# Graph attention layers on one core: transfers taken off GpSimd, and the last product's rows finished at other steps

## The chip, the core and the metric

The kernel runs on one core of a Trainium2 chip. The metric is device time in microseconds (us) of one execution, from start to end; smaller is better. The engines of the core are named as the profile names them: PE (TensorE, matrix products and transposes), DVE (VectorE, elementwise work), ACT (ScalarE, activations and scaled copies), POOL (GpSimd) and SP (SyncE, which here only issues transfers). SP, ACT and POOL can each issue DMA transfers; an engine takes its instructions in order, so a transfer that has to wait holds up what stands behind it on that engine.

## The reference

Two layers over a graph of 3327 nodes with 512 features. The adjacency is used three times: added to the attention scores (twice, as spatial and as edge encoding), and as A2 = adj + I in two products.

```python
h = jnp.maximum(_layernorm(x), 0.0)                    # layer 0
q, k, v = h @ Wq.T + bq, h @ Wk.T + bk, h @ Wv.T + bv
a = q @ k.T / sqrt(512) + adj + adj
x = x + softmax(a, axis=-1) @ v
h = jnp.maximum(_layernorm(x), 0.0)                    # layer 1
A2 = adj + eye
d = diagonal(A2) ** -0.5
temp = A2 @ h @ W.T
x = x + relu((d[:, None] * A2 * d[None, :]) @ temp)
```

## The kernel before

Rows are padded to 26 tiles of 128. All matrix work is in 32-bit floats, and all large products use a scheme of seven block products in place of eight: sums and differences of the blocks are formed first (DVE), seven products are accumulated in seven PSUM banks (PE), and the results are combined afterwards (DVE). The kernel has these stages.

- **Projection** (0 to about 100 us). x is loaded tile by tile (L275), normalised, and its ReLU `ht` is stored as `rowd[0]` (L324) and transposed on PE. The query side is projected and stored as `qd` (L362).
- **Scores** (about 100 to 640 us). Four groups of 13 steps. A step loads two tiles of adjacency, `g`, for the step after the next (L418), runs seven products for its pair of tiles (L454), adds them to twice the adjacency (L458, L466), and takes the exponential on ACT (L461, L468). Beside this, DVE forms the sums of adjacency for the next step (L440), which are stored as `sumd` (L446), and block sums of the exponentials of the step before, which are stored as `pd` in four pieces (L462, L481, L485, L490). The tiles `g` are reused after four steps, so a load must wait until these stores have landed. The order on DVE, PE, POOL and SP is held to that of the program by `in_order`. At the end the row totals are stored (L514) and loaded again in another layout (L573).
- **Three products** (about 640 to 2190 us), numbered g = 0, 1, 2: exponentials times h, A2 times the second h, A2 times temp. A product consists of seven block products r in the order p5, p1, p6, p7, p2, p3, p4. Each goes over two strips s of output columns, 14 and 12 tiles wide, and each strip over seven steps t: six with a pair of row tiles (L801) and a seventh with the one left over (`t is None`, L793). That makes 294 steps, about 5.4 us each, and `number_of(g, r, s, t)` is a step's number. `Step.load` fetches left tiles three steps ahead, `Right.load` the rows of the right side five steps ahead. After the sixth step `Gather.first` copies a bank to SBUF on ACT (L829) and combines four banks on DVE (L830 to L833); after the seventh `Gather.rest` adds the others (L846 to L849, or L843 for the very last strip), and `Gather.settle` folds the strip into the output `cts` (L857 to L862).

The work beside the products hangs on step numbers: `at(k, what)` puts a task into `between`, and `within` holds tasks that run inside a step after its fourth matmul. Tasks whose name contains "load" run at the beginning of the step. These tasks matter here:

- `Job` (L872 on) forms more sums of adjacency and stores them (L887); `Right.make` stores a part of the right side for later use (L766).
- `attend` and `attended` finish the rows of layer 0: they store the residual `x1d` (L907) and the second h, `rowd[1]` (L913). `Temp.product` makes temp and stores it as `rowd[2]` (L963).
- `finish` writes the result of one tile of rows: four transposes from `cts` into a bank (L987), a ReLU with scale on ACT (L989), the residual added on DVE (L990), and the store (L92). `finish_load` fetches the residual from `x1d` (L970), and `last_load` does it for the last rows (L977). All of these transposes but the last go to one bank, the role "p8", so a transpose must wait until ACT has emptied it. Rows 0 to 19 are finished whole during the block products p3 and p4 of the last product. Rows 20 to 25 are finished in halves: the second half of their columns early in block product p2 (step (4, 0, t)), the first half after everything else.

In the kernel before, POOL issues all stores but four of the last. The residual buffers come from a ring of four (`xr_ring`), the output buffers from one of four (`out_ring`).

Of the kernel before, what the change touches and what calls it, by code (L numbers as in the profile page):

```python
# [47 lines left out]
def graph_layers_kernel(  # L48
# [41 lines left out]
    def store(dst, src, n, queue=nc.gpsimd):  # L90
        for a, z in pieces(n):
            queue.dma_start(dst[a:z], src[a:z])  # L92
# [223 lines left out]
    def h_transposed(k):  # L316

        a, n = PACKS[k]
        for _, i in (o for o in order if o[0] == k):
# [4 lines left out]
            nc.gpsimd.dma_start(rowd[0][ROW[i]], ht)  # L324
# [13 lines left out]
    def project_q(k):  # L338
# [5 lines left out]
        def chain(o):  # L344
# [12 lines left out]
            def last():  # L357
                if o == 1:
                    for j in range(4):
                        y, z = divmod(j, 2)  # L360
                        i = ROW[y * HALF + a] * P
                        nc.gpsimd.dma_start(qd[:, 2 * z : 2 * z + 2, i : i + w], qs[j][:, :, :w])  # L362
# [58 lines left out]
    class Pair:  # L421
# [11 lines left out]
        def sum_of_adjacency(self, m):  # L433
# [11 lines left out]
            if m == 1:  # L445
                nc.gpsimd.dma_start(self.to(sumd)[:, 0:2], self.o)  # L446

        def multiply(self, qt):
# [8 lines left out]
            def first(n, ps, sign):  # L457
                nc.vector.scalar_tensor_tensor(a[n], a[n], 2.0, ps[:, :wd], op0=ALU.mult,  # L458
                                               op1=ALU.add if sign > 0 else ALU.subtract)
                if n == 2:  # L460
                    nc.scalar.activation(g[1], g[1], AF.Exp, **({"bias": pad} if self.t == HALF - 1 else {}))  # L461
                    nc.gpsimd.dma_start(self.to(pd)[:, 0:2], g[1])  # L462
# [15 lines left out]
        def s1(self):  # L478
            s1 = self.g[0][:, 1]
            nc.vector.tensor_add(s1, s1, self.g[1][:, 1])  # L480
            nc.gpsimd.dma_start(self.to(pd)[:, 2:4], self.g[0])  # L481

        def s2(self):
            nc.vector.tensor_add(self.e[:, 1], self.g[0][:, 0], self.g[0][:, 1])
            nc.gpsimd.dma_start(self.to(pd)[:, 4:6], self.e)  # L485

        def s4(self):
            self.last = fours[:, self.t % 2, : self.wd]
            nc.vector.tensor_add(self.last, self.e[:, 1], self.g[1][:, 0])
            nc.gpsimd.dma_start(self.to(pd)[:, 6], self.last)  # L490
# [11 lines left out]
        def total(self, m, own=None):  # L502
# [11 lines left out]
            nc.gpsimd.dma_start(totd[:, c0 : c0 + self.wd], row)  # L514
# [55 lines left out]
    def totals():  # L570
        for m in range(2):
            pairs[len(steps_of_scores) - 1].total(m, bank(ROLE["p8"], "tot"))
        nc.sync.dma_start(tot, totd[0].rearrange("(i p) -> p i", p=P))  # L573
# [110 lines left out]
    cts = {}  # L684

# [15 lines left out]
    xr_ring = ring(*spare[:3], (half, 14))  # L701
    out_ring = ring((half, 12), (half, 13), *spare[3:])
# [24 lines left out]
    class Right:  # L727
# [31 lines left out]
        def make(self):  # L759
# [3 lines left out]
            if r == "p6":  # L763
                yield nc.vector.tensor_add(own, own, self.two[:, :, 0:E])
                yield nc.vector.tensor_sub(own, own, self.two[:, :, E:D])
                nc.gpsimd.dma_start(self.t2[:, 0 : 2 * self.n], self.b[:, 0 : 2 * self.n])  # L766
# [39 lines left out]
    class Gather:  # L806
# [31 lines left out]
        def rest(self, ps):  # L838
            p = {k: ps[k][:, : self.width] for k in ("p2", "p3", "p4", "p8")}
            if self.last:  # L840
                flags.append(nc.values_load(bad, min_val=0, max_val=1))  # L841
                for o, k in zip(self.parts(self.regions[2]), p):
                    nc.vector.tensor_add(o, o, p[k])  # L843
# [25 lines left out]
    class Job:  # L869
# [13 lines left out]
        def make(self):  # L883
# [3 lines left out]
            nc.gpsimd.dma_start(sumd[self.s][self.j][:, 2 + self.k], self.a)  # L887
# [14 lines left out]
    def attend(i):  # L902
# [4 lines left out]
        nc.gpsimd.dma_start(x1d[i], xt)  # L907
        normed[i] = norm(xt)

    def attended(i):  # L910
        h1 = h_ring([P, D], "h1")
        nc.scalar.activation(h1, xts[i], AF.Relu, bias=normed[i][1](), scale=normed[i][0])
        nc.gpsimd.dma_start(rowd[1][i], h1)  # L913
# [13 lines left out]
    class Temp:  # L927
# [18 lines left out]
        def product(self, j):  # L946
# [14 lines left out]
            if j == len(PARTS) - 1:  # L961
                for i, ts in zip(self.its, self.to):
                    nc.gpsimd.dma_start(rowd[2][i], ts)  # L963
# [3 lines left out]
    def finish_load(i, z=(0, 1)):  # L967
        c0, c1 = z[0] * E, (z[-1] + 1) * E
        xrs[i] = xr_ring([P, D], "xr")
# [9 lines left out]
    def finish(i, z=(0, 1), spot=None, queue=nc.gpsimd):  # L979

        s, y, k = where(i)
# [3 lines left out]
        pt = bank(ROLE["p8"] if spot is None else spot, "pt")  # L985
        for d in range(c0 // P, c1 // P):
            nc.tensor.transpose(pt[:, d * P : (d + 1) * P], cts[s][y][d][:, k * P : (k + 1) * P], ident)  # L987
# [3 lines left out]
        store(out[i * P : i * P + n, c0:c1], o[:n, c0:c1], n, queue)  # L991
# [32 lines left out]
    def rows(g, k, i, *z):  # L1024
# [5 lines left out]
        else:  # L1030
            at(k - 1, finish_load, i, *z)
# [21 lines left out]
    for (n, s, t), its in {  # L1053
        (5, 1, 2): (0,), (5, 1, 3): (1,), (5, 1, 4): (2,), (5, 1, 5): (3,),
        (6, 0, 0): (4,), (6, 0, 1): (5,), (6, 0, 2): (6, 17), (6, 0, 3): (14, 18), (6, 0, 4): (15, 19), (6, 0, 5): (16,),
        (6, 1, 2): (7, 8), (6, 1, 3): (9, 10), (6, 1, 4): (11, 12), (6, 1, 5): (None, 13),
    }.items():
        for i, when in zip(its, (between, within)):
            if i is not None:
                k = number_of(2, n, s, t)  # L1060
                at(k - 1, finish_load, i)
                when.setdefault(k, []).append((finish, (i,)))
    for t, i in enumerate(range(20, NT)):
        rows(2, number_of(2, 4, 0, t), i, (1,))
    for n, i in enumerate(range(20, NT, 2)):
        at(number_of(2, 6, 1, 2) + n, last_load, i)
    for k, what in ((1, totals), (2, prepare), (6, prepared), (8, judge), (9, judged)):
# [32 lines left out]
    def run(k):  # L1100
        step = steps[k]
# [18 lines left out]
        for j, _ in enumerate(itertools.chain((None,), step.multiply(banks_of))):  # L1120
# [11 lines left out]
            elif weighs and j > 0:  # L1132
                do(first_of(waiting), 2)
        if t is None:
            do(first_of(waiting))
            gatherer.rest(banks_of)
# [13 lines left out]
    with in_order(*(e.engine for e in (nc.vector, nc.tensor, nc.gpsimd, nc.scalar, nc.sync))):  # L1150
        for k in range(len(steps)):
            run(k)
        for n, i in enumerate(range(20, NT)):
            finish(i, (0,), (0, 2, 4, 6, 7, 1)[n], (nc.gpsimd, nc.sync)[n % 2])
# [376 lines left out]
```

## Time and profile before

| What | us |
|---|---|
| median of 3 runs | 2209.17 |
| lowest and highest | 2204.41, 2212.06 |
| the profiled execution, its own time | 2208.99 |
| its span, from the first to the last instruction | 2207.1 |
| TensorE busy in the span | 2172.1 (98%) |
| VectorE busy | 1664.2 (75%) |
| ScalarE busy | 238.4 (11%) |
| GpSimd busy | 357.2 (16%) |
| mean granted TensorE clock | 0.993 of full speed |
| DMA: 583.71 MB moved, mean | 264 GB/s |

A line of instructions gives the source line, the engine, the operation, the tile written and the tiles read, and how long it took; idle time before it stands in brackets, with what ended it. A "q" behind an engine's name means its sequencer, which issues transfers and waits, and isn't counted as busy. For PE, weight loads are listed apart as PEld. An FP32 matmul of the program shows as two records. The granted clock is the share of full speed that the chip's throttle let PE have in a stretch.

### The profile page before, as it was taken

The numbers are of one execution on the slowest core, as the hardware profiler recorded it, in microseconds if no ns is written. First come the engines' busy times: TensorE is split into PE (matmuls) and PEld (weight loads), VectorE is DVE, ScalarE is ACT, GpSimd is POOL, SyncE is SP. The second block draws the span as 40 slices with busy tenths as digits, with TensorE's granted clock in tenths as the row PEclk, the third lists the DMA queues.
The fourth block names the chain that finished last, engine by engine and source line by source line (L and its number), as shares of the span: only waits on it lengthen the run. The fifth ranks groups of instructions, "written<-read, shape, count | busy, mean of one in ns | idle before, by whom it ended". The sixth has DMA issues, their size and how long they took to land. (4 is left out here: it accounts for less than half of the span.)

```text
span 2207.1 us, 21499 instructions
## 1 busy us (share of the span) xinstructions
PE 2172.1 (98%) x6424; PEld 1198.7 (54%) x6424; DVE 1664.2 (75%) x3250; ACT 238.4 (11%) x363; POOL 357.2 (16%) x551
## 2 busy tenths in 40 slices
PE   9999999999999999999999999999999999999997
PEld 6555555455545555555454555555666655555554
DVE  6369888888877788777777778886667577876775
ACT  5311121112110000000001000000111100000011
POOL 5233333333321000001222100000000000000011
PEclk9999999999999999999999999999999999999999
DMA  8568888888969898889787889886645458766684
GB/s 288 186 221 296 293 296 287 302 283 311 359 214 326 308 373 293 274 291 318 254 307 266 302 325 347 290 291 202 217 149 187 142 193 304 235 210 186 208 294 151
DMA packets 247196, 583.71 MB, mean 264 GB/s; under 512 B 34768, under 2 KB 107294, under 8 KB 247070
## 3 DMA queue, kind: packets, MB, share of 16 engines
q1 hardware_dynamic: 192782, 399.28, 53.9%
q0 software_dynamic: 44928, 167.49, 20.1%
q10 hardware_dynamic: 9360, 15.47, 2.2%
q8 instruction: 53, 0.87, 0.2%
q14 instruction: 73, 0.60, 0.1%
HBM read 414.28 MB, written 167.85 MB: 264 GB/s over the span
## 5 line engine op out<-in xcount | busy, mean ns | idle before, releaser
L801 PE MATMUL p<-part,b 128*128 128x448 f32 (+1 forms) x3528 | 1268.6, 515 | 5.0 <-DVE part L174 4.9
L801 PEld LDWEIGHTS p<-part,b 128*128 128x128 f32 x3528 | 670.4, 191 | 544.3 <-issue 287.6
L454 PE MATMUL Y<-qt,hp 128*128 128x448 f32 (+1 forms) x832 | 308.8, 513 | 2.4 <-DVE g L458 1.5
L173 DVE TENSOR_TENSOR part<-part 128x896 f32<-128x896 f32 (+1 forms) x252 | 256.8, 1019 | 61.0 <-DMA part<-p 26.4
L454 PEld LDWEIGHTS Y<-qt,hp 128*128 128x128 f32 x832 | 157.3, 190 | 137.7 <-issue 72.3
L454 PE MATMUL Z<-qt,hp 128*128 128x384 f32 (+1 forms) x416 | 162.5, 513 | 0.0
L175 DVE TENSOR_TENSOR part<-part,part 128x448 f32<-128x448 f32 (+1 forms) x219 | 129.4, 591 | 14.9
L174 DVE TENSOR_TENSOR part<-part,part 128x448 f32<-128x448 f32 (+1 forms) x219 | 129.4, 591 | 7.2
L793 PE MATMUL p<-part,b 128*128 128x448 f32 (+1 forms) x336 | 124.2, 513 | 0.0
L454 PEld LDWEIGHTS Z<-qt,hp 128*128 128x128 f32 x416 | 78.8, 190 | 67.4 <-issue 37.4
L458 DVE SCALAR_TENSOR_TENSOR g<-g,Y 128x384 f32<-128x384 f32 (+1 forms) x156 | 91.3, 585 | 29.2 <-PE Y L454 28.1
L887 POOL DMA_DIRECT2D sum<-job x52 | 28.4, 547 | 503.9 <-DVE job L884 285.9
L793 PEld LDWEIGHTS p<-part,b 128*128 128x128 f32 x336 | 63.6, 190 | 53.1 <-issue 31.3
L829 ACT COPY part<-p 128x384 f32<-128x384 f32 (+1 forms) x33 | 16.6, 503 | 669.4 <-PE p L801 669.4
L454 PE MATMUL X<-qt,hp 128*128 128x384 f32 (+1 forms) x208 | 81.1, 512 | 0.0
L461 ACT ACTIVATE g<-g 128x768 f32<-128x768 f32 (+1 forms) x48 | 43.0, 896 | 351.4 <-DVE g L458 299.3
L446 POOL DMA_DIRECT2D sum<-o x52 | 36.8, 709 | 218.8 <-DVE o L440 150.3
L92 POOL DMA_DIRECT2D out_dram<-r x30 | 16.2, 542 | 309.3 <-DVE r L990 269.0
L830 DVE TENSOR_TENSOR part<-p,part 128x384 f32<-128x384 f32 (+1 forms) x33 | 19.3, 585 | 59.5 <-PE p L801 58.8
L893 PE MATMUL p<-w,ct 128*128 128x512 f32 x136 | 61.8, 594 | 0.4 <-DVE part L905 0.4
L454 PEld LDWEIGHTS X<-qt,hp 128*128 128x128 f32 x208 | 39.5, 190 | 33.1 <-issue 19.3
L954 PE MATMUL pw<-w,rows 128*128 128x256 f32 x208 | 53.6, 380 | 0.8 <-DVE rows L944 0.8
(191 smaller groups left out, 2048.6 us busy)
## 6 DMA issues: line engine op xcount, KB each, us to landing
part<-sum SPq DMA_DIRECT2D x104, 448.0 KB, 5.2
part<-p SPq DMA_DIRECT2D x91, 448.0 KB, 6.1
part<-sum SPq DMA_DIRECT2D x104, 384.0 KB, 3.5
part<-p SPq DMA_DIRECT2D x91, 384.0 KB, 4.2
part<-in_adjT_dram SPq DMA_DIRECT2D x78, 448.0 KB, 4.7
b<-row SPq DMA_DIRECT2D x234, 128.0 KB, 4.9
part<-in_adjT_dram SPq DMA_DIRECT2D x78, 384.0 KB, 3.6
g<-in_adjT_dram SPq DMA_DIRECT2D x52, 448.0 KB, 4.4
```

What stands on the lines that cost most here:

```text
L173: yield nc.vector.tensor_add(o[:, 0:2], g[:, 0:4:3], g[:, 1:2].to_broadcast([P, 2, g.shape[-1]]))
L174: yield nc.vector.tensor_add(o[:, 2], o[:, 1], g[:, 0])
L175: yield nc.vector.tensor_add(o[:, 3], o[:, 2], g[:, 2])
L446: nc.gpsimd.dma_start(self.to(sumd)[:, 0:2], self.o)
L454: nc.tensor.matmul(ps[:, :wd], h_of(self.t, name, k), qt[B[name]][:, k], start=start and k == 0, stop=k == 1, skip_group_check=True)
L458: nc.vector.scalar_tensor_tensor(a[n], a[n], 2.0, ps[:, :wd], op0=ALU.mult, op1=ALU.add if sign > 0 else ALU.subtract)
L461: nc.scalar.activation(g[1], g[1], AF.Exp, **({"bias": pad} if self.t == HALF - 1 else {}))
L793: yield nc.tensor.matmul(ps[("p2", "p3", "p4", "p8")[k]][:, :w], b[:, z], a[:, 0, y], start=k == 3, stop=True)
L801: yield nc.tensor.matmul(ps[r][:, :w], b[:, i], m, start=self.t == 0, stop=self.t == PAIRS - 1 and r in ("p1", "p5", "p6", "p7"))
L887: nc.gpsimd.dma_start(sumd[self.s][self.j][:, 2 + self.k], self.a)
L893: nc.tensor.matmul(ps, cts[s][y][d][:, k * P : (k + 1) * P], w[d], start=d == 0, stop=d == DC - 1)
L954: nc.tensor.matmul(ps, a, W[B[name]][:, c], start=new and c == 0, stop=c == 1, skip_group_check=True)
```

## The change

- No transfer is issued by POOL any more. Stores of the projection and of the scores go to SP; stores of the products go to ACT.
- Stores of the products are not issued where they are recorded. `post` (and `finish` by itself) puts them on a list, and `deliver(k)`, called in step k after its matmuls, issues those that were recorded in steps before k. Only `attended` issues its store at once. At the end SP issues the last rows' stores, but for two that ACT issues.
- The load of the row totals is a task of its own, `load_totals`, at step 3; it stood at the end of `totals` at step 1.
- Residual buffers come from a ring of seven, output buffers from one of five, and `finish_load` runs two steps ahead of `finish` instead of one.
- The rows 0 to 19 are finished at other steps of p3 and p4 (the table of `within`), and the second half of the columns of rows 20 to 25 two steps later.
- For the last six rows, `rest` is split: the adds of p2 and p3, then the transposes of rows 20 to 22 (`turn_last`), then the adds of p4 and p8 and the transposes of rows 23 to 25. Before, all four adds came first, and each row's transposes were followed by its evictions.

The diff, cut to its core (the one-word changes of a queue's name are shown once for each target):

```diff
-    def store(dst, src, n, queue=nc.gpsimd):
+    def store(dst, src, n, queue=nc.scalar):
...
-            nc.gpsimd.dma_start(rowd[0][ROW[i]], ht)
+            nc.sync.dma_start(rowd[0][ROW[i]], ht)
...
             pairs[len(steps_of_scores) - 1].total(m, bank(ROLE["p8"], "tot"))
+
+    def load_totals():
         nc.sync.dma_start(tot, totd[0].rearrange("(i p) -> p i", p=P))
...
+    now = [0]
+    posted = []
+
+    def post(dst, src):
+        posted.append((now[0], lambda: nc.scalar.dma_start(dst, src)))
+
+    def deliver(before):
+        while posted and posted[0][0] < before:
+            posted.pop(0)[1]()
...
-    xr_ring = ring(*spare[:3], (half, 14))
-    out_ring = ring((half, 12), (half, 13), *spare[3:])
+    xr_slots = [lambda k=k: view(2, 1).rearrange("p a w -> p (a w)")[:, k * D : (k + 1) * D] for k in range(3)]
+    xr_slots = itertools.cycle([*xr_slots, *(lambda f=f, k=k: f(k, [P, D], "xr") for f, k in (*spare[:3], (half, 14)))])
+    out_ring = ring(*((half, k) for k in (11, 12, 13)), *spare[3:])
...
-            nc.gpsimd.dma_start(sumd[self.s][self.j][:, 2 + self.k], self.a)
+            post(sumd[self.s][self.j][:, 2 + self.k], self.a)
...
-        nc.gpsimd.dma_start(rowd[1][i], h1)
+        nc.scalar.dma_start(rowd[1][i], h1)
...
+    def turned(i, z, spot):
         s, y, k = where(i)
+        pt = bank(spot, "pt")
+        for d in range(z[0] * DC // 2, (z[-1] + 1) * DC // 2):
+            nc.tensor.transpose(pt[:, d * P : (d + 1) * P], cts[s][y][d][:, k * P : (k + 1) * P], ident)
+        return pt
+
+    turned_last = {}
+
+    def turn_last(i):
+        turned_last[i] = turned(i, (0,), LAST[i - 20])
+
+    LAST = tuple(ROLE[p] for p in ("p6", "p7", "p5", "p2", "p3", "p1"))
+
+    def finish(i, z=(0, 1), spot=None, queue=nc.scalar):
+
         n = min(P, N - i * P)
...
-        pt = bank(ROLE["p8"] if spot is None else spot, "pt")
-        for d in range(c0 // P, c1 // P):
-            nc.tensor.transpose(pt[:, d * P : (d + 1) * P], cts[s][y][d][:, k * P : (k + 1) * P], ident)
+        pt = turned(i, z, ROLE["p8"]) if spot is None else turned_last[i]
...
-        store(out[i * P : i * P + n, c0:c1], o[:n, c0:c1], n, queue)
+        posted.append((now[0], lambda: store(out[i * P : i * P + n, c0:c1], o[:n, c0:c1], n, queue)))
...
-            at(k - 1, finish_load, i, *z)
+            at(k - 2, finish_load, i, *z)
...
-        (5, 1, 2): (0,), (5, 1, 3): (1,), (5, 1, 4): (2,), (5, 1, 5): (3,),
-        (6, 0, 0): (4,), (6, 0, 1): (5,), (6, 0, 2): (6, 17), (6, 0, 3): (14, 18), (6, 0, 4): (15, 19), (6, 0, 5): (16,),
-        (6, 1, 2): (7, 8), (6, 1, 3): (9, 10), (6, 1, 4): (11, 12), (6, 1, 5): (None, 13),
+        (5, 1, 1): (0,), (5, 1, 2): (1,), (5, 1, 3): (2,), (5, 1, 4): (3,), (5, 1, 5): (4,),
+        (6, 0, 1): (5,), (6, 0, 2): (6, 14), (6, 0, 3): (15, 16), (6, 0, 4): (17, 18),
+        (6, 1, 1): (19, 7), (6, 1, 2): (8, 9), (6, 1, 3): (10, 11), (6, 1, 4): (12, 13),
...
-        rows(2, number_of(2, 4, 0, t), i, (1,))
+        rows(2, number_of(2, 4, 0, t + 2), i, (1,))
...
-    for k, what in ((1, totals), (2, prepare), (6, prepared), (8, judge), (9, judged)):
+    for k, what in ((1, totals), (3, load_totals), (2, prepare), (6, prepared), (8, judge), (9, judged)):
...
+        deliver(k)
         if t is None:
             do(first_of(waiting))
-            gatherer.rest(banks_of)
+            if gatherer.last:
+                flags.append(nc.values_load(bad, min_val=0, max_val=1))
+                for n, names in enumerate((("p2", "p3"), ("p4", "p8"))):
+                    gatherer.rest(banks_of, names)
+                    for i in range(20 + 3 * n, 23 + 3 * n):
+                        turn_last(i)
+            else:
+                gatherer.rest(banks_of)
...
+        deliver(len(steps))
+        now[0] = len(steps)
         for n, i in enumerate(range(20, NT)):
-            finish(i, (0,), (0, 2, 4, 6, 7, 1)[n], (nc.gpsimd, nc.sync)[n % 2])
+            finish(i, (0,), LAST[n], nc.scalar if n in (3, 4) else nc.sync)
+        deliver(len(steps) + 1)
```

## The prediction

> **What bounds the kernel now.** I read in this order: the busy shares, the stretches of the end one by one, the order of time on TensorE (PE), ScalarE (ACT) and VectorE (DVE) around each idle stretch, the waits of SyncE (SP), and the lines at which the program closes. The page first:
>
> ```profile
> span 2207.1 us, 21499 instructions
> PE 2172.1 (98%) x6424; PEld 1198.7 (54%) x6424; DVE 1664.2 (75%) x3250; ACT 238.4 (11%) x363; POOL 357.2 (16%) x551
> q0 software_dynamic: 44928, 167.49, 20.1%
> ```
>
> PE is the bound: 35 us of the span are left, 1.1 before the first matmul, 14.1 after the last transpose (2192.92), 19.7 in between. Work that PE must do isn't touched, so only these 35 us, and PE's own time at half clock, can be won; any wait that reaches PE is lost. The stretches of the end (columns: length, busy time of PE, PEld, DVE, ACT, POOL, granted clock, DMA share, GB/s):
>
> ```profile
> 1978.00:1984.30 6.30, 3.22 (x10) 1.38 (x9) 6.14 (x8) 0.00 (x0) 0.00 (x0) 1.00 0.75 259
> 1984.30:1992.00 7.70, 7.70 (x19) 3.84 (x19) 7.32 (x18) 0.78 (x2) 0.54 (x1) 0.78 0.34 105
> 2126.60:2133.50 6.90, 3.63 (x15) 2.17 (x14) 5.42 (x12) 0.69 (x1) 1.08 (x2) 0.88 0.72 216
> 2133.50:2139.50 6.00, 6.00 (x14) 2.92 (x13) 4.54 (x10) 0.69 (x1) 1.08 (x2) 0.56 0.53 166
> 2195.10:2207.10 12.00, 0.00 (x0) 0.00 (x0) 0.00 (x0) 0.00 (x0) 0.01 (x1) 0.57 0.15 44
> ```
>
> Twice PE idles and then works at a reduced clock; for the last 12 us nothing computes. The two idle stretches in order of time (in brackets: idle before, and who ended it):
>
> ```profile
> 1984.14 0.33 PE L987 MATMUL pt<-ident,part 128*128 128x128 f32 x1 [2.53 <-DVE part L859]
> ...
> 2126.43 5.36 ACTq L970 DMA_DIRECT2D xr<-x1d  x2
> 2130.75 0.68 DVE L990 TENSOR_TENSOR r<-r,xr 128x512 f32<-128x512 f32 x1
> 2131.89 0.69 ACT L989 ACTIVATE r<-pt,sd 128x512 f32<-128x512 f32 x1 [7.50 <-DVE r L990]
> 2132.63 1.12 PE L987 MATMUL pt<-ident,ct 128*128 128x128 f32 x4 [3.27 <-ACT r L989]
> ```
>
> First: a transpose of a finished row waits for the settling sums (L857-859) of that very strip. Second: ACT issues two residual loads, the second stands 5 us until DVE's add (L990) frees its buffer; the ReLU behind it on ACT is late, so the one bank for transposes stays full and PE stands. Then the waits of SP and the closing instructions:
>
> ```profile
> SPq L418 <- DMA p<-g: 441.1, 48, 48.2
> L573 SPq EVENT_SEMAPHORE  x1: 25733/25733/25733, 625.7 to 625.7; - x1
> L1523 POOLq DRAIN  x3: 40/107/5459, 2200.8 to 2206.8; - x3
> L1527 POOLq INC_SWDGE_SEM  x1: 1512/1512/1512, 2199.2 to 2199.2; - x1
> DMA to landing us min/median/max: 2.0/3.4/6.0
> ```
>
> In scores SP's loads of adjacency wait for the landing of the stores of two steps before. At the end GpSimd (POOL) alone spends 1.51 us on its counter and 5.46 us on a drain while all others stand; the last line is of the stores of the result (L92).
>
> **What the skill says.** "TensorE: Matmul & The Clock Gate", Part 1: The HAM clock gate: an idle window of about 3.4 us halves the clock, and the window runs free. The trace agrees: clock 0.56 after 3.27 us of idling, 0.78 after 0.56 and 2.53. "DMA: Bandwidth & Descriptors", SWDGE vs HWDGE vs iDMA: all issuing engines feed the same 16 DMA engines, and a separate queue saves only time at issue. The trace agrees in that a byte costs about the same from either queue: 20.1% for POOL's 167.49 MB against 53.9% for SP's 399.28 MB, so 12% more from SP. No page has a price for the drain.
>
> **The change part by part.** The order of both built programs shows 491 transfers on POOL before and none after; SP goes from 1185 to 1496, ACT from 65 to 245; the counts of arithmetic on PE, DVE, ACT and POOL are equal.
>
> 1. Rows 20-25, first columns, two steps later (t+2), loads at k-2. The settling sums ended at 1984.08; a step here is about 5.4 us, so the transposes come some 9 us after what held them. Gone: 0.56 + 2.53 = 3.09 idle, and 7.7 x (1 - 0.78) = 1.7 of clock: 4.8 us. Price if the cover fails: the same again.
>
> 2. Residual ring from 4 to 7, loads at k-2, output ring from 4 to 5, rows spread anew. A load at step k now needs the add of seven rows ago, where DVE was late by about one step; two rows a step make that over three steps. Gone: 3.27 idle, and half of the 6.1 us from 2132.63 to about 2138.7 that ran at half clock, 3.05: 6.3 us. The other waits of this kind (0.35 at 2182) add 0.3. What is late next is VectorE (9.96 of 12.9 us busy in the two stretches from 2126.6), by less than a step. If a store on ACT waits in the loads' place, one such stall returns: 6.3.
>
> 3. The last rows in halves. The last matmul ended at 2190.75 (2188.01 + 2.74), transposes began at 2191.39 after all four adds. Now the upper half's two adds are done before that matmul ends, so ACT's six evictions, 0.36 apart, start 0.64 earlier. Gain 0.6; bounds 0 and 1.0 (two adds of 0.49).
>
> 4. The close without POOL. The last store was issued at 2195.06 and landed 4.2 us later; SP's waits up to 2199.73 and its 12 waits from 2200.7 to 2201.4 would have ended it, then two barriers of together 0.8 (2206.27 to 2207.06). POOL's counter and drain stood between. After: landing, 0.5 + 0.7 + 0.1 + 0.8 = 2.1 us, against 7.8 (2199.26 to 2207.06): gain 5.7. POOL's last work is then a norm's power (L200, before 1240 us), so a drain that remains lies beside PE. If the drain must still run last, the gain is 0.3. The last landing: one such store alone took 2.08 from SP, the last of seven together 4.2; I take 3.5, gain 0.7, bounds 0 and 2.1.
>
> 5. Stores of scores on SP: five a step of 10.5 us. SP issued a load here in 0.39 us, so 2 us of issue in a queue that stood 402 of 440 us for landings. Queued behind a store that waits for DVE or ACT are the next loads (L418), and for these DVE's adjacency sums (L440), the scores' updates behind them, PE. Cover: a load issued at 303.2 landed at 307.83 and was read at 315.03: 7.2 us. The loads wait for the landing of these stores anyway, and stores stand in the program's order, before the next loads, as on POOL. DMA share: 0.83 in scores; stores are half of that, at 12% more per byte 0.88-0.89, so landings lengthen by perhaps 1 us, well inside. Cost 0; bounds -1 and +7.
>
> 6. Stores of products on ACT: 52 sums, 21 of the right side, 26 residuals, 26 + 26 rows and most of the output: some 180 x 0.33-0.45 = 70 us of issue in 1550 us in which ACT is busy for under a tenth. They're handed over a step later than computed, so their data is ready; behind them stand the copy L829, which waited 669 us for PE, and the evictions L958 and L989. Cost 0; bounds 0 and +4.
>
> 7. The totals' load two steps later: SP no longer stands 25.7 us at L573 for a landing, though it now stands for DVE's total before it can store it (649.9 against 651.4). Four idles of PE here, 0.58, 0.87, 0.96 and 0.64, are late loads and sums; I take 1.0 of the 3.05, bounds 0 and 3.
>
> 8. First stage: 26 row stores and 16 query stores on SP among the loads of x. PE idles 2.5 us in the first 100; cost 0, bounds -1 and +3.
>
> Sum: 4.8 + 6.3 + 0.3 + 0.6 + 5.7 + 0.7 + 1.0 = 19.4 us. The profiled execution took 2209.0 us, and the median of the runs is 2209.2, so no correction: 2189.6.
>
> **Rivals.**
> - The stall or the close comes back in part: one wait of point 2's kind in ACT's queue (+6.3), or the drain still last (+5.4). For it: ACT issues in order, and I can't see what the drain waits for. Against: seven slots, and no transfer of POOL is left. 2195-2196; with both 2201.
> - Lost elsewhere: points 5 to 8 at their bad bounds (7 + 4 + 1 + 3 = 15) leave 4 us: 2205, no change that can be told.
> - Slower: in scores, load, sum, store and load again now share one queue in order. It decides once a load lands over 11.8 us after its issue (315.03 - 303.2). Then each us beyond is paid in nearly every one of 52 steps: 1 us late costs some 50, less 19 won: 2240. For it: SP waits 402 us for exactly these landings, and DMA is at 0.83 already. Against: 4.6 us is what a load takes, with 7.2 to spare.
> - It isn't done: excluded by the order, no transfer is left on POOL.
>
> **How the numbers follow.** Chances: the forecast (2182-2195) 0.62, a part comes back (2195-2202) 0.20, lost elsewhere 0.07, slower 0.11. The range reaches from the sum with good bounds (landing 1.4 more, point 7 2.0, others 2-4: 2182) to the second case's end with a little of the third: 2203. About 0.3% (6.6 us) is what a measurement of this kernel can tell from no change; beyond it on the fast side lie the first two cases: faster 0.82, same 0.07, slower 0.11.
>
> **What would show it.** Right: no half clock between 1950 and 2195; under 1 us of idle of PE before any transpose of a finished row; the span ends 9 to 10 us after the last matmul (16.3 before) and POOL's long drain, if there is one, lies far earlier; scores as long as before within 3 us. Wrong: DVE's L440 waiting for g in most steps, ACT's evictions waiting behind its own stores, or POOL still closing last.

## The result and the profile after

| What | before, us | after, us |
|---|---|---|
| median of 4 runs | 2209.14 | 2187.01 |
| lowest and highest | 2204.41, 2212.06 | 2183.81, 2190.65 |
| the profiled execution, its own time | 2208.99 | 2190.65 |
| its span | 2207.1 | 2188.9 |

The ratio is 0.9902, with a 95% interval of 0.9878 to 0.9927: 22.1 us less, between 16 and 27. The prediction had 19.4 less, 2189.6. The profiled execution of the changed kernel is the slowest of its four, so a later profile of the same kernel (after_again, 2185.35) stands beside it where that matters.

The page of the changed kernel, span, busy shares and DMA queues:

```profile
span 2188.9 us, 21095 instructions
...
PE 2168.6 (99%) x6424; PEld 1198.7 (55%) x6424; DVE 1665.0 (76%) x3250; ACT 238.8 (11%) x363; POOL 48.6 (2%) x60
...
q1 hardware_dynamic: 265102, 512.76, 69.5%
q10 hardware_dynamic: 35150, 69.48, 8.7%
```

The counts on PE, DVE and ACT are what they were. POOL has lost its 491 transfers, the software queue is gone, and SP (q1) and ACT (q10) carry its bytes. The end of the last product and the close, in stretches (length, busy time of PE, PEld, DVE, ACT, POOL, granted clock, DMA share, GB/s):

```profile
1950.00:2035.00 85.00, 83.94 (x253) 46.37 (x252) 65.20 (x113) 3.86 (x8) 0.00 (x0) 1.00 0.70 218
2035.00:2120.00 85.00, 85.00 (x261) 46.89 (x260) 62.35 (x116) 5.62 (x9) 0.00 (x0) 1.00 0.78 260
2120.00:2179.12 59.12, 59.12 (x212) 34.57 (x211) 48.13 (x89) 10.60 (x16) 0.00 (x0) 1.00 0.67 230
2179.12:2188.90 9.78, 1.42 (x13) 1.06 (x10) 2.81 (x7) 2.30 (x6) 0.00 (x0) 0.82 0.28 89
```

From 2035 to the last matmul PE has no idle at all and the full clock; the only idle left there is 1.06 us at 1955, which was there before. From the last matmul to the end it takes 9.7 us (16.3 before); this stretch is called the close below. When PE reaches the same points of the program tells where the time went:

| PE reaches | before | after | after_again |
|---|---|---|---|
| the totals' matmul (L507) | 648.16 | 648.08 | 645.22 |
| the matmul of the last product's p7 that waits there | 1955.20 | 1955.68 | 1950.55 |
| the end of the last matmul | 2190.75 | 2179.12 | 2173.99 |
| the end of the program | 2207.06 | 2188.86 | 2183.57 |

In both profiles 12.1 us are won between 1955 and the last matmul, and 6.6 to 6.7 behind it. What differs between them lies before 1955: the first won nothing there, the second 4.7 us. Of these 5.1 us of difference, 2.9 lie before the totals' matmul, where the first idles 1.7 us more at 634 and has a window of 3.4 us at half clock behind that. The other 2.3 lie between 650 and 1955: another such window at 878, and 0.58 us of idle at 1339, both absent in the second.

The waits of SP that point 5 asked about, and POOL's drains at the close (x, shortest/median/longest in ns, first and last start):

```profile
SPq L418 <- DMA p<-g: 110.4, 47, 6.3
```

```profile
L1557 POOLq DRAIN  x3: 34/45/82, 1239.9 to 2188.6; - x3
```

SP stands 110 us for the landings of the stores of g instead of 441. It now issues these stores itself, and stands for their data before that instead: some 190 us at L446, L462, L481 and L485. DVE's L440 never waits for g. No drain takes longer than 82 ns.

### The profile page after: what moved, and what is told of

Same layout as the page of the kernel before. It is cut to its first block, busy times and chain, and to the rows that moved or that the text cites. A ratio compares the mean times of both kernels' runs of the same rounds, so it can differ in the third digit from the quotient of the medians.

```text
span 2188.9 us, 21095 instructions
## 1 busy us (share of the span) xinstructions
PE 2168.6 (99%) x6424; PEld 1198.7 (55%) x6424; DVE 1665.0 (76%) x3250; ACT 238.8 (11%) x363; POOL 48.6 (2%) x60
## 4 chain that ended last, share of the span: by engine, by line
PE 93%; DVE 4%; DMA 2%; issue 1%; SPq 0%; ACT 0%; POOL 0%; DVEq 0%; POOLq 0%
PE p L813 52%; PE Y L454 13%; PE Z L454 7%; PE p L805 5%; PE p L905 4%; PE pw L966 3%; PE X L454 3%; PE Y L347 2%; PE Z L347 1%; DVE part L173 1%; DMA part<-sum 1%; PE mm L306 1%; PE tp L327 1%; PE pt L995 1%; PE X L347 0%
## 5 line engine op out<-in xcount | busy, mean ns | idle before, releaser
L200 POOL TENSOR_TENSOR rstd<-ve,mhalf 128x1 f32<-128x1 f32 x52 | 42.7, 823 | 572.1 <-DVE ve L198 541.8
L896 DVE TENSOR_TENSOR job<-job 128x896 f32<-128x896 f32 (+1 forms) x52 | 53.0, 1019 | 0.0
L466 DVE TENSOR_TENSOR g<-g,Z 128x384 f32<-128x384 f32 (+1 forms) x52 | 30.5, 586 | 27.0 <-PE Z L454 26.7
```

The source lines that it names most:

```text
L896: nc.vector.tensor_add(self.a, self.a, self.b)
```

## The experiments

Twelve runs follow, eleven of other kernels and one of the changed kernel again. Times are medians of four runs (13 in one case); "chip 1", "chip 2" and "chip 3" are the three groups that shared a chip and its runs of the kernel before (medians 2207.73, 2209.68 and 2208.82).

### The two halves of the change (chip 1)

**stores_only**: the changed kernel with rings, tables, steps and the last adds as before.

```diff
-            at(k - 2, finish_load, i, *z)
+            at(k - 1, finish_load, i, *z)
...
-        rows(2, number_of(2, 4, 0, t + 2), i, (1,))
+        rows(2, number_of(2, 4, 0, t), i, (1,))
...
-                for n, names in enumerate((("p2", "p3"), ("p4", "p8"))):
-                    gatherer.rest(banks_of, names)
-                    for i in range(20 + 3 * n, 23 + 3 * n):
-                        turn_last(i)
+                gatherer.rest(banks_of)
```

> The kernel before with only its stores moved off GpSimd (SyncE in projection and scores, ScalarE in the products through the list, SyncE and ScalarE at the end); rings, tables of rows, totals' load and the adds of the last rows as before. Theory of the prediction (points 4 to 6): the close gains 6.4 us (5.7 without counter and drain, 0.7 of landing) and the queues cost nothing, so 2209.1 - 6.4 = 2202.7; both idle stretches of the last product (some 3 us each, with half clock behind) stay. Rival A, the gain of the whole change lies in the schedule and the new queues give a part back: 2205 to 2209. Rival B, the stores' queue was itself a cause of the stalls: below 2199, and the idle before the transposes at 2130 shrinks below 2 us.

**schedule_only**: the kernel before with the new steps, rings and tables, and nothing else.

```diff
-    xr_ring = ring(*spare[:3], (half, 14))
-    out_ring = ring((half, 12), (half, 13), *spare[3:])
+    xr_slots = [lambda k=k: view(2, 1).rearrange("p a w -> p (a w)")[:, k * D : (k + 1) * D] for k in range(3)]
...
+    out_ring = ring(*((half, k) for k in (11, 12, 13)), *spare[3:])
...
-        rows(2, number_of(2, 4, 0, t), i, (1,))
+        rows(2, number_of(2, 4, 0, t + 2), i, (1,))
```

> The kernel before, stores still by GpSimd, with the new steps alone: residual ring of seven and loads two steps ahead, output ring of five, the new table of rows, rows 20 to 25 two steps later, the totals' load at step 3. Theory (points 1, 2 and 7): 4.8 + 6.3 + 0.3 + 1.0 = 12.4 less, 2196.7; no idle over 1 us before a transpose of a finished row, and the close still 16 us from the last matmul to the end, with the drain of 5 us. Rival: stalls return through the output buffers, which are freed by GpSimd's slower stores: idle over 2 us before a transpose, 2202 or more.

Measured: stores_only 2196.88 (ratio 0.9943, 0.9926 to 0.9960), schedule_only 2195.87 (0.9945, 0.9929 to 0.9962). By medians 10.9 and 11.9 less: together 22.7, so within the intervals the halves add up to the whole's 22.1. The second agrees with its 12.4. From the wait at 1955 to the last matmul schedule_only takes 223.4 us, as the changed kernel does, stores_only 233.4 and the kernel before 235.5. So the 12.1 us of this stretch belong to the new steps and rings.

The first won more than the 6.4 that I had given to the stores; its interval begins at 8.8. By its time, below 2199, it went to rival B. By its trace it didn't: near 2130 it idles 4.0 us in three pieces (0.94, 2.04 and 1.03), more than the 3.27 before, though no window at half clock follows. Its trace is 10.3 us shorter than that of the kernel before: 6.5 at the close, 2.2 between 1955 and the last matmul, and 1.7 before 1955. What lies before 1955 was the next question. Its trace holds a second surprise, at the very end. Before the change (in order of time; the group of four adds brings the last four banks into the rows):

```profile
2189.37 1.97 DVE L843 TENSOR_TENSOR part<-part,p 128x384 f32<-128x384 f32 x4
...
2191.39 1.53 PE L987 MATMUL pt<-ident,part 128*128 128x128 f32 x12 [0.65 <-DVE part L843]
```

The same place in stores_only, where the four adds still stand together:

```profile
2184.79 2.10 PE L802 MATMUL p<-part,b 128*128 128x384 f32 x6
...
2185.51 1.97 DVE L852 TENSOR_TENSOR part<-part,p 128x384 f32<-128x384 f32 x4
...
2186.72 1.57 PE L992 MATMUL pt<-ident,part 128*128 128x128 f32 x12
```

The adds end at 2187.48, yet the transposes begin at 2186.72 without idle. So the 0.65 us did not hang on the order of the adds. What stores_only keeps of the change there is the list of banks: before, row 20, the first, was transposed into bank 0, where the last product's p8 lies until the fourth add has read it; `LAST` gives that bank to row 25, the last. schedule_only, which keeps the list of before, keeps the 0.65 us too. No run changed the list alone, so this cause is read from the code; that it isn't the halves is shown.

### What the drain waits for (chips 1 and 2)

**last_on_pool**, **three_last_on_pool**: one, or three, of the last stores by POOL in the changed kernel. **first_on_pool**: one early store. **scores_on_pool**: all stores of projection and scores.

```diff
-            finish(i, (0,), LAST[n], nc.scalar if n in (3, 4) else nc.sync)
+            finish(i, (0,), LAST[n], nc.gpsimd if n == 4 else nc.scalar if n == 3 else nc.sync)
```

> The changed kernel with one of the seven last stores (row tile 24) issued by GpSimd; no other transfer by GpSimd. Theory: any software transfer still open at the end brings the counter and the drain back behind the last landing: 5.4 to 7 us more than the changed kernel, 2192.5 to 2194, with a drain of about 5 us that runs last. Rival: the drain's length comes from the many transfers before (491 in the kernel before): with a single one it takes under 1 us, and the time is within 2 us of the changed kernel's 2187.

```diff
-            nc.sync.dma_start(rowd[0][ROW[i]], ht)
+            (nc.gpsimd if i == 0 else nc.sync).dma_start(rowd[0][ROW[i]], ht)
```

> The changed kernel with one early store (the first tile's h in the projection) issued by GpSimd, all else as in the changed kernel. Theory: the drain waits only for GpSimd's own work to end, so it runs near 1240 us beside TensorE: within 1.5 us of the changed kernel's 2187. Rival: counter and drain stand behind the barrier at the end whenever the program has one software transfer: 5.4 to 7 us more, 2192.5 to 2194, with the drain last.

```diff
-            finish(i, (0,), LAST[n], nc.scalar if n in (3, 4) else nc.sync)
+            finish(i, (0,), LAST[n], (nc.gpsimd, nc.sync)[n % 2])
```

> The changed kernel with the last six rows' stores given out as before the change (rows 20, 22 and 24 to GpSimd, the others to SyncE); no other transfer by GpSimd, so three in all. Theory: the long drain belongs to the many transfers that GpSimd has issued over the execution, not to late ones; with three there is no counter, the drain ends with the landing, as with one, and from the last matmul to the end it takes 8 to 10 us: time within 2 us of the changed kernel. Rival: it belongs to late software stores, and one of them was too few to show it: counter and a drain of 5 us at the end, 12.5 us or more from the last matmul to the end, 2191 or more.

```diff
-            nc.sync.dma_start(rowd[0][ROW[i]], ht)
+            nc.gpsimd.dma_start(rowd[0][ROW[i]], ht)
...
-                nc.sync.dma_start(self.to(sumd)[:, 0:2], self.o)
+                nc.gpsimd.dma_start(self.to(sumd)[:, 0:2], self.o)
...
-            nc.sync.dma_start(self.to(pd)[:, 2:4], self.g[0])
+            nc.gpsimd.dma_start(self.to(pd)[:, 2:4], self.g[0])
```

> The changed kernel with the stores of the projection and of the scores back on GpSimd, none of them later than the scores; products' and last stores as in the changed kernel. Theory: counter and long drain come back (many transfers), but right behind GpSimd's last work near 1240 us, beside TensorE, so that the close stays at 8 to 10 us and the time within 3 us of the changed kernel. Rival: they stand behind the closing wait of SyncE whenever there were many software transfers: 5 us or more after the last landing, 2192 or more.

| Kernel | transfers by POOL | longest drain behind POOL's work, us | its start | from the last matmul to the end, us | median, us |
|---|---|---|---|---|---|
| before | 491 | 5.46 (and 1.51 of counter) | 2200.8 | 16.3 | 2209.1 |
| schedule_only | 491 | 5.46 (and 1.52) | 2188.8 | 15.9 | 2195.87 |
| scores_on_pool | 310, the last at 651 | 4.89 | 1239.8 | 10.0 | 2191.94 |
| rows_of_h_on_pool (below) | 42, the last at 125 | 3.50 | 1239.7 | 10.9 | 2188.53 |
| three_last_on_pool | 3 | 2.29 | 2179.9 | 10.3 | 2185.85 |
| last_on_pool | 1 | 2.85 | 2177.1 | 10.8 | 2185.69 |
| first_on_pool | 1, the first | 0.14 | 1239.3 | 9.7 | 2187.6 |
| after | 0 | 0.08 | 2188.3 | 9.7 | 2187.01 |

The drains of scores_on_pool, and then of three_last_on_pool:

```profile
L1557 POOLq DRAIN  x3: 44/107/4892, 1239.8 to 2188.5; - x3
```

```profile
L1557 POOLq DRAIN  x3: 40/113/2286, 2179.9 to 2186.5; - x3
```

My theory for last_on_pool, that any late software transfer brings the drain back, fell. With one late store the drain ends at 2179.91, 0.1 us after that store's landing, while SP's own stores are still under way, so it isn't what ends the program. Nor is a cost shown: the closes with one or three late transfers by POOL, 10.8 and 10.3 us, lie within the 9.5 to 10.9 of the nine traces that have the changed close and no late transfer by POOL. A drain of 5 us belongs to the many transfers issued before, and stands right behind POOL's own last work: with 310 transfers it takes 4.89 us at 1240, beside PE, and costs nothing. first_on_pool went as its theory said. The kernel before had both, many transfers and a last one at the very end. Its trace shows POOL itself waiting for its landings, then the counter, and then the drain; no close of a kernel with 310 transfers or fewer has the counter.

By its time scores_on_pool went to the rival (some 6 us over three_last_on_pool and rows_slot, the kernels of chip 2 that keep all of the new schedule), by its drain to the theory: what it lost lies elsewhere, before 650 us.

### The stores of the projection (chip 3)

Without the wait for the first matmul, PE idled 5.7 us before 650 in scores_on_pool; on the same chip it was 3.2 in three_last_on_pool and 1.3 in ring_undone and rows_slot. Two of these stretches lie at 55 and 98, as in the kernel before. The kernel before in order of time:

```profile
50.76 1.24 POOL L324 DMA_DIRECT2D row<-ht  x2 [0.73 <-ACT ht L323]
...
52.02 1.08 POOL L200 TENSOR_TENSOR rstd<-ve,mhalf 128x1 f32<-128x1 f32 x2
...
52.62 0.16 DVE L204 SCALAR_TENSOR_TENSOR nb<-mv,rstd 128x1 f32<-128x1 f32 x1 [2.08 <-ACT hp L332]
...
54.50 1.06 PE L327 MATMUL tp<-ident,ht 128*128 128x128 f32 x8 [0.66 <-DVE nb L204]
```

The kernel after, at the same tiles:

```profile
51.77 0.55 POOL L200 TENSOR_TENSOR rstd<-ve,mhalf 128x1 f32<-128x1 f32 x1 [5.41 <-DVE hp L334]
...
52.35 0.16 DVE L204 SCALAR_TENSOR_TENSOR nb<-mv,rstd 128x1 f32<-128x1 f32 x1 [0.59 <-POOL rstd L200]
```

POOL computes a power for each norm (L200), and its stores stood in front of it; the norm, ht and the transposes behind it were late. (The bracket at L204 names ACT, whose copy ended at about the same time; what L204 reads is the power, which ended at 52.58.) After the change POOL is idle 5.4 us and takes the power at once. The second stretch hangs on a landing: SP's wait in scores_on_pool between 80 and 100,

```profile
SPq L399 <- DMA qd<-qs: 8.8, 1, 8.8
```

is for a store of queries that POOL issued right behind a store of sums and that landed 6.4 us after its issue. To settle the part of the projection:

```diff
-            nc.sync.dma_start(rowd[0][ROW[i]], ht)
+            nc.gpsimd.dma_start(rowd[0][ROW[i]], ht)
...
-                        nc.sync.dma_start(qd[:, 2 * z : 2 * z + 2, i : i + w], qs[j][:, :, :w])
+                        nc.gpsimd.dma_start(qd[:, 2 * z : 2 * z + 2, i : i + w], qs[j][:, :, :w])
```

> The changed kernel with the stores of the projection alone (26 of h, 16 of queries) back on GpSimd; the scores' stores stay on SyncE. Theory, new after the runs so far: GpSimd computes the power of each norm (L200) in the projection, and its own stores stood in front of it; so TensorE's busy time from 50 to 100 us falls from 49.8 back to about 48.1 with idle near 54 and 96, and the time rises by 1.5 to 2 us; the rest of scores_on_pool's loss belongs to the scores. Rival: these idles come from the DMA traffic of the scores' stores or from chance: TensorE's busy time in that stretch stays over 49.5.

| Kernel | PE busy from 50 to 100, us | idle at 54 to 56 | idle at 96 to 98 | median, us |
|---|---|---|---|---|
| before | 48.15 | 0.66 | 1.19 | 2209.1 |
| scores_on_pool | 47.98 | 0.67 | 1.34 | 2191.94 |
| schedule_only | 49.33 | 0.67 | none | 2195.87 |
| rows_of_h_on_pool | 49.33 | 0.68 | none | 2188.53 |
| after | 49.85 | none | none | 2187.01 |

Half right: the first stretch comes back with the projection's stores alone. It stands in all five traces with these stores on POOL, and in none of the nine others. The second doesn't come back: there the sums are stored by SP, the queries' store on POOL lands after 2.9 us, and nothing is late. But a store of sums by POOL in front is not enough to make it late: schedule_only has it, and the queries land after 4.1 us. A rival is that the stores wait behind SP's loads of g. In the three traces with this idle the last of these loads lands at 88.8 to 89.8, in schedule_only at 86.9, and in all four the store of sums lands 0.8 to 1.0 us behind it. No run parts the two, so the cause of the second stretch stays open.

The time rose by 3.2 us against the changed kernel on the same chip, more than these 0.7 us; the trace also shows 1.50 us of idle at 634, of which more below.

The scores' stores have a stretch of their own. In all four traces with these stores on POOL, DVE's L440 stands 3.5 to 5.6 us between 570 and 600 for transfers that haven't landed (1.80 and 1.12 for g at 575 and 577 in the kernel before), and PE idles 0.6 to 2.3 us between 575 and 610. The ten others show neither.

### Single steps of the schedule

**rows_only** (chip 3): the kernel before with one edit.

```diff
-        rows(2, number_of(2, 4, 0, t), i, (1,))
+        rows(2, number_of(2, 4, 0, t + 2), i, (1,))
```

> The kernel before with one edit: the second half of rows 20 to 25 finished two steps later. Theory (point 1): 4.8 us less than before, of which 3.1 are idle before the transposes at 1981 to 1985 and 1.7 the half clock behind it; the idle near 2130 and the close stay. Rival: VectorE is late by more than two steps there and the wait only moves: less than 2 us gained, idle over 1 us before these transposes.

Measured over 13 runs: 2203.6, ratio 0.9976 (0.9968 to 0.9985), 5.2 less. No idle over 0.25 us between 1957 and 2129; the idle of 3.28 at 2129 and the close of 16.3 stay. The wait went and nothing took its place.

**ring_undone** (chip 2): the changed kernel with both rings and the loads as before, undone together; the new table stays.

```diff
-        xrs[i] = next(xr_slots)()
+        xrs[i] = xr_ring([P, D], "xr")
...
-                at(k - 2, finish_load, i)
+                at(k - 1, finish_load, i)
```

> The changed kernel with the residual ring of four, the output ring of four and the loads of residuals one step ahead again; the new table of rows stays, and so do the stores on ScalarE. Theory (point 2): the ring and the earlier loads carry the gain, so most of 6.3 us comes back: idle of 2 us or more before a transpose of a finished row around 2130, 2191 to 2194. Rival: the new table alone spreads the rows enough, so under 1 us of idle before any transpose, and within 2 us of the changed kernel.

Measured: 2191.05, 5.2 and 5.6 over the two other kernels of chip 2 that keep the rings, three_last_on_pool and rows_slot. Its order of time:

```profile
2113.94 7.93 ACTq L981 DMA_DIRECT2D xr<-x1d  x2
...
2120.83 0.68 DVE L1012 TENSOR_TENSOR r<-r,xr 128x512 f32<-128x512 f32 x1
2121.92 0.69 ACT L1011 ACTIVATE r<-pt,sd 128x512 f32<-128x512 f32 x1 [7.30 <-DVE r L1012]
...
2122.66 1.12 PE L994 MATMUL pt<-ident,ct 128*128 128x128 f32 x4 [3.06 <-ACT r L1011]
```

It is the stall of before, link by link: the second residual load stands on ACT until DVE's add frees its buffer, the ReLU behind it is late, PE stands 3.06 us. With a second idle of 0.84 us at 2166 and half of the 3.4 us at half clock behind the stall, that makes 5.6 us. The new table alone doesn't spread the rows enough; the rival fell. What the residual ring, the output ring and the earlier loads are worth one by one was not measured.

### The idle that comes and goes, and a faster version

The profiled execution of the changed kernel idles at 634, more than before the change:

```profile
632.09 0.69 DVE L774 TENSOR_TENSOR b<-rows 128x512 f32<-128x512 f32 x1 [3.36 <-DMA rows<-row]
...
634.43 1.69 PE L454 MATMUL Y<-qt,hp 128*128 128x384 f32 x4 [2.21 <-DVE g L466]
```

DVE stands for rows of the first product's right side, with sums that PE needs behind it. The buffer of these rows is one that the last group of scores reads until about 625, so SP can load it no earlier: it issues the load between 624.1 and 625.3 in all eight traces with these buffers and SP's stores in scores. These show an idle of 2.21, 1.97, 0.50, 3.68, 1.65, 1.50 and 0.50 us, and once none. **rows_slot** (chip 2) gives the rows a buffer that is free by then:

```diff
-    b_ring = ring(*((half, k) for k in (0, 1, 2, 3, 8, 9, 10)))
-    r_ring = ring(*((half, k) for k in (4, 5, 6, 7)))
+    b_ring = ring(*((half, k) for k in (0, 1, 2, 7, 8, 9, 10)))
+    r_ring = ring(*((half, k) for k in (4, 5, 6, 3)))
```

> The changed kernel with two half-size buffers swapped: the fourth of the right side's row buffers was one that the last group of scores still reads, and is now one that is free by then (its partner goes to a buffer that no load has to wait for). Theory: the idle before a product of scores near 634 us (0.5 to 3.7 us in three looks at the same code, and half clock behind it in two of them) comes from VectorE standing for rows that SyncE could load only at 625; with the buffer free the load goes out earlier, this idle falls under 0.6, and the time falls by 2 to 4 us against the changed kernel, about 2184. Rival: the loads land late because the DMA engines are full there, whatever their issue: the idle stays 1 us or more, and the time within 1 us of 2187.

```profile
625.61 0.68 DVE L774 TENSOR_TENSOR b<-rows 128x512 f32<-128x512 f32 x1
...
630.68 1.56 PE L454 MATMUL Y<-qt,hp 128*128 128x384 f32 x4
```

DVE takes the rows at 625.6, without a wait (632.1 and 630.9 in the two profiles of the changed kernel; in the eight traces it waits 0.95 to 4.82 us), and PE has no idle over 0.25 us from 26 to 643. settle_split, which has the same buffers, shows the same. The median, 2185.48, is within what the measurement can tell from the changed kernel (2187.01, 2185.29), so the stall went and the gain of 2 to 4 us isn't shown by the times. The four runs lie within 1.8 us.

**settle_split** (chip 3) has the buffers of rows_slot and adds an edit for the idle that is left in the products: of the six settling sums after p7, three are done a step later, behind the sums of adjacency that PE needs, and a job that would fall into that step moves on by one.

```diff
-            waiting.append(gatherer.settle())
+            settle = gatherer.settle()
+            if step.r == "p7":
+                waiting.append(itertools.islice(settle, 3))
+                later.append(settle)
+            else:
+                waiting.append(settle)
```

> The changed kernel with the buffers of rows_slot, and two edits more: of the six settling sums after block product p7 three are done a step later, behind the sums of adjacency for the next product, and a job that falls into the step of these sums is moved one step on. Theory: the idle before products at 878, 1422, 1454 and 1955 (1.93, 1.06, 0.86 and 1.06 us) is VectorE's settling in front of sums that TensorE needs; all four fall under 0.3, 4.9 us less, with the rows' stall 6 to 9 less than the changed kernel on the same chip: 2178 to 2181. Rival: VectorE has no slack there and the idle only moves a step on: less than 2 us beyond rows_slot, 2183 or more.

**after_again** is the changed kernel as it is.

> The changed kernel as it is, for a comparison on one chip with the three others. Theory: 2184 to 2189, with idle near 634 us that differs from one execution to the next; from the last matmul to the end 9 to 10 us. Rival: the first measurement was of a chip that favours it, and the time is over 2191.

Measured on chip 3: after_again, as expected, 2185.29 (2183.63 to 2186.43), settle_split 2178.39 (2175.48 to 2179.47; ratio to before 0.9859, 0.9843 to 0.9875). The ranges don't overlap: 6.9 us less than the changed kernel, within what was expected, and the fastest version here. PE around the three places, first in settle_split, then in after_again:

```profile
860.00:900.00 40.00, 40.00 (x121) 22.73 (x120) 36.23 (x58) 0.48 (x1) 0.00 (x0) 1.00 0.84 287
1400.00:1460.00 60.00, 60.00 (x175) 32.76 (x174) 53.93 (x89) 0.48 (x1) 0.00 (x0) 1.00 0.87 303
1940.00:1960.00 20.00, 20.00 (x63) 11.78 (x63) 16.33 (x25) 0.48 (x1) 0.00 (x0) 1.00 0.74 230
```

```profile
860.00:900.00 40.00, 38.07 (x115) 21.45 (x114) 33.49 (x52) 0.48 (x1) 0.00 (x0) 1.00 0.83 285
1400.00:1460.00 60.00, 58.08 (x168) 31.43 (x167) 52.53 (x88) 0.48 (x1) 0.00 (x0) 1.00 0.85 295
1940.00:1960.00 20.00, 18.94 (x59) 10.91 (x58) 17.88 (x27) 0.00 (x0) 0.00 (x0) 1.00 0.63 192
```

1.93 + 1.92 + 1.06 = 4.91 us of idle are gone. Against them stand 0.63 us at 1315, which no other trace has, and 0.71 at 1332, at a matmul where seven other traces idle 0.4 to 0.8 us and after_again by chance doesn't. The two profiles are 5.9 us apart; half of 3.4 us that settle_split spends less at half clock near 25 us, which its edits don't touch, is part of that.

## Why the prediction came out

The forecast case held: 2187.0 against 2189.6. Its points, one by one:

| Point | predicted, us | what the runs show |
|---|---|---|
| 1 rows 20 to 25 later | 4.8 | 5.2 (3.3 to 7.1), rows_only |
| 2 rings, loads, table | 6.6 | 5.2 to 5.6, ring_undone (without the table) |
| 1 and 2 together | 11.4 | 12.1, from 1955 to the last matmul |
| 3 last rows in halves | 0.6 | 0.65, but not from the halves |
| 4 close and last landing | 6.4 | with point 3: 16.31 to 9.74, so 6.6 of 7.0 |
| 5 and 8 scores and first stage | 0 | 1.85 of idle gone at 54 and 96, 0.58 at 578: 2.4 |
| 6 products' stores on ACT | 0 | no loss seen |
| 7 totals' load | 1.0 | none seen |

- **Points 1 and 2** were right in mechanism and size. (Point 1 names the first columns; what moves is the second half of the columns, and its sum doesn't hang on that.) The chain of the stall was reproduced by undoing the rings and the earlier loads. Their price in half clock was an estimate on top of the idle, and that part is chance: in rows_only the same idle of 3.28 brought one window of 3.4 us at half clock, in the kernel before one of 6.8; that makes 1.7 us of difference at the same stall.
- **Point 3** was right in size and wrong in cause. It said that the upper half's adds being done early starts the transposes earlier. stores_only keeps the adds together and starts them just as early. I had read the list of banks in the diff and not asked which bank the last add still reads.
- **Point 4**: the close fell to 9.7 us, in the 9 to 10 that I gave. Of the open question, what the drain waits for, this much is answered: it is long where POOL has issued many transfers, and it follows POOL's own last work. The landing took 3.2 us (from 2183.70 to SP's wait ending at 2186.94; predicted 3.5), but the last issue was not earlier for it. SP's second store here took 1.87 us to issue, so that the last went out 4.6 us after the last matmul (4.3 before):

```profile
2178.96 1.57 PE L995 MATMUL pt<-ident,part 128*128 128x128 f32 x12
2179.38 2.30 ACT L1012 ACTIVATE r<-pt,sd 128x256 f32<-128x256 f32 x6 [6.19 <-PE pt L995]
2179.89 1.89 DVE L1013 TENSOR_TENSOR r<-r,xr 128x256 f32<-128x256 f32 x5 [0.17 <-ACT r L1012]
2180.34 2.31 SPq L92 DMA_DIRECT2D out_dram<-r  x2
```

- **Points 5 and 8** are the term that was mis-sized. I priced what SP would have to issue more, and forgot what POOL would have to issue less: its stores stood in front of the norms' powers (0.66 us), and DVE's waits for g near 575, which I had feared from SP's one queue, stood in the kernel before and went (0.58). The cause of the 1.19 us at 96 is open. With the measured sizes the sum is 5.2 + 5.4 + 6.6 + 2.4 = 19.6, and that it comes so near the forecast's 19.4 is in part luck: 2.4 that I did not foresee stand against point 7's 1.0 and 1.2 too much in points 1 to 4. With the traces' 12.1 in place of 5.2 + 5.4 it is 21.1; what is left to the medians' 22.1 lies inside the result's interval. after_again's profile, 23.5 us shorter than that of the kernel before, shows chance in the clock as well: it spends 10.2 us less at half clock, of which the 3.4 at 878 come and go.
- **Point 7** failed. The idle of 0.64 at 648 is in every trace, with the load at step 1 or 3, and schedule_only, which has the new step, keeps the idle of 0.9 to 1.0 us at 633 and 636. The idle near 632 to 636 had another cause, the buffer of the right side's rows (in the kernel before DVE waits 2.40 us for them at 630.9), which rows_slot took away.

Left open: why a store's issue on SP takes 0.35 us once and 1.87 the next time; no run was made for it. It is no accident of one execution: all eleven traces with the changed close have one issue of 1.2 to 1.9 us on SP there, the three with the old close none. In eight of them a long issue on ACT ends within 0.02 us of it, as if both queues waited for one thing. How much of the spread of 7 us among the runs of the changed kernel is the idle at 634 isn't settled either, since each run has only one profiled execution.

## What to carry to other kernels

When transfers leave an engine, look at the engine they leave as well as at the one they go to: arithmetic that stood behind them in order comes earlier. Before you price a wait on a result, ask which buffer or bank the waiting instruction writes, and who still reads it; three of the stalls here (the residual ring, bank 0, the rows' buffer) were of that kind. Software transfers (those that POOL issues) needn't be banned for their closing cost: here the drain of many of them was free where POOL's last work was early, and three or fewer late ones showed no cost.

## What was not expected of the hardware

- The drain's length goes with the number of transfers that POOL has issued: 5.46 us with 491 (the same in all three kernels), 4.89 with 310, 3.50 with 42, 0.14 with a single early one. It isn't in proportion, and the runs don't part their number from their bytes. With one or three late ones it was 2.85 and 2.29, and ended 0.1 to 0.2 us behind their landing.
- An idle of 1.93 us near 878 stands in all 13 traces of kernels with this code (all but settle_split). In 4 of them a window of 3.4 us at half clock follows within about 1 us, in 9 none. The Trainium skill, "TensorE: Matmul & The Clock Gate", Part 1: The HAM clock gate, says that the window runs free, which fits the chance, and puts the half rate after at least one idle window of about 3.4 us; here an idle of little more than half of that was enough at times, and the measurement decides. The 2.53 us before the window at 1985 in the kernel before, which the prediction took for agreement, are below it too.
- The same store of queries by POOL landed 2.9, 4.1 or 6.4 us after its issue (rows_of_h_on_pool, schedule_only, the kernel before). In the last two a store of sums went out just ahead, and both stores landed soon behind SP's loads of g: at 87.9 and 88.8 behind 86.9 in schedule_only, at 89.5 and 90.5 behind 88.8 in the kernel before. Which of the two it hangs on isn't shown.
